# An output of lane X gives way to the closing of a block where fewer than 28 groups of scores are ready

## The chip, the cores and the metric

The kernel runs on one core of a Trainium2 chip. The metric is the device time of one execution in microseconds; the time of a kernel is the median over its runs. The core has five engines that each work through a queue of their own, in the order in which the program was recorded: TensorE (PE, its weight loads PEld), VectorE (DVE), ScalarE (ACT), GpSimd (POOL) and SyncE (SP), which here issues nearly all DMAs.

## What is computed

Four images of 128 channels and 64x64 pixels go through two layers. The first is a convolution block with a selective scan (Mamba), the second attention over the 4096 pixels of an image with 4 heads of 32, and a mixture of 8 experts of which each pixel takes 2:

```python
x = x + _L0_conv_ref(_gn(x), ...)          # norm, 3x3 conv, gelu, scan over 4096 steps, projection
t = _to_tokens(x)
t = t + _L1_attn_ref(_ln_t(t), W_qkv, b_qkv, W_proj, b_proj)
t = t + _L1_ffn_ref(_ln_t(t), router_w, router_b, expert_w, expert_b)
x = _from_tokens(t, x)
```

Attention of one image needs the whole first layer of that image: the scores of a query block against a key block can be made as soon as both blocks have left the scan and were projected. The output of a query block (projection, routing, experts) can be made when all eight key blocks of 512 pixels have been summed.

## The kernel before

An image (a batch b) is cut into 8 blocks of 512 pixels. The instructions of all engines are written down by one Python loop (line 1362), and `queued` (line 389) fixes that order on each engine, so the loop is the schedule. One pass of the loop is a slot. Two slots make a unit: a scan over two of the 16 states of half the channels of a block. A block has 2 x 8 units, so 32 slots; the 32 blocks of the four images fill 1024 slots (`END`). Each block of 32 slots in the loop is called a block of the loop below, with a slot in it from 0 to 31.

Beside the scan, a slot takes three kinds of work:

- One group of scores from the generator `attention` (line 912): two key tiles against 1024 queries of one head. Four matmuls make the scores (`sc`), two exponentials follow (`pT`, in `exponentials`), and in the next slot four matmuls, recorded by the profiler as eight, sum the values (`av`, in `weighted`). There are 1024 groups. `RUNS` fixes their order: pairs of query blocks against ranges of key blocks. A part is one head of such a pair against one or two key blocks, 2 or 4 groups. `ready` (line 908) asks whether the blocks that a part needs have been closed; where they have not, the generator yields nothing and the slot goes without scores. The keys, queries and values of a part are loaded from DRAM, for the next part three groups ahead where it is ready by then.
- Steps of lane Y (up to two per slot): the norm, the convolution and the inputs of the scan of the coming blocks, in a fixed order. At the sixth block of an image the group statistics of the next image come too.
- Steps of lane X (up to two per slot): closings and outputs. A closing (`closed`, line 793) takes the block that the scan has just left through the projections, and stores its keys, queries and values; it is put at the head of the lane as soon as the scan of the block has ended, about slot 2 of the next block of the loop, and takes ten slots. An output (`finished`, line 1032) takes a query block whose sums are complete through projection, routing and the 8 experts, in sixteen slots. Outputs are appended to the lane by `inverted` (line 1012).

Lane X runs one task at a time. `advance` (line 1254) lets an output start only in slots 2 to 17 of a block of the loop:

```python
if (
    tasks[0][0][0] == "out" and slot < END + 4
    and not 2 <= slot % (2 * NST) < NST + 2
):
    return False
```

In slot 2 the scan's last product of the old block has not been handled yet, so an output that waits is taken first, in slots 2 to 17, and the closing of the block follows in slots 17 to 26. Where no output waits, the closing starts in slot 3. After slot 1024 there is no scan; the loop goes on until the remaining scores, closings and outputs are done, with outputs on both lanes. Followed through the counters of the loop, the recorded program has 1194 slots, of which 170 take no scores: slots 0 to 78, 83 to 110, 131 to 142 and 199 to 206 at the start, 383 to 384, 653 to 654 and 911 to 912 where one image's attention gives way to the next, 409 to 412, 469 to 476, and the last 25.

Of the kernel before, what the change touches and what calls it, by code (L numbers as in the profile page):

```python
# [21 lines left out]
NT = BLK // P  # L22
IMG = 64
DI = 64
NST = 16
# [11 lines left out]
def conv_mamba_attn_moe_kernel(ctx: ExitStack, tc: tile.TileContext, t: dict):  # L37
# [374 lines left out]
    def mm(out, lhsT, rhs, start=True, stop=True):  # L412
        tensor.matmul(out, lhsT=lhsT, rhs=rhs, start=start, stop=stop)
# [456 lines left out]


    STEP = 2

    def queries(b, qp, h):

        qs = att.tile([P, 2 * BLK], F32R, name="qs", bufs=2)
        src = kqv[b][1][qp][DH * h : DH * h + DH].rearrange("d a r l -> (d a r) l")
        sync.dma_start(out=qs.bitcast(F32), in_=src)
        return qs

    def keys(b, h, k, u, n):

        ks = att.tile([P, 2 * BLK], F32R, name="ks", bufs=3)
        src = kqv[b][0][k][DH * h : DH * h + DH].rearrange("d a l -> (d a) l")
        src = src[:, u * BLK : (u + n) * BLK]
        sync.dma_start(
            out=ks[:, : n * BLK].bitcast(F32),
            in_=src[:, None, :].to_broadcast([2 * DH, 2, n * BLK]),
        )
        return ks  # L890

    def values(b, h, k, u, n):
        v = att.tile([P, 2, NT, 2 * DH], F32, name="v", bufs=3)
        sync.dma_start(
            out=v[:, :n].rearrange("p i j d -> p i (j d)"),
            in_=kqv[b][2][k][h, u : u + n].rearrange("i p q -> p i q"),
        )
        return v
# [9 lines left out]
    def ready(b, part):  # L908
        last = max(2 * part[0] + 1, 2 * part[2] + part[3] + part[4] - 1)
        return all(("closed", b, i) in done for i in range(last + 1))  # L910

    def attention(b):

        seen, parts = {}, []
        for q, lo, hi in RUNS:
            known = seen.get(q, 0)
            seen[q] = known + hi - lo  # L920
            cuts = [lo, *range(lo + 2 - lo % 2, hi, 2), hi]
            for h in range(NH):
                for k0, k1 in zip(cuts, cuts[1:]):
                    parts.append((
                        q, h, k0 // 2, k0 % 2, k1 - k0, k0 == lo, k1 == hi, known > 0,
                        seen[q] == NB,
                    ))
        assert all(n == NB for n in seen.values())

        def load(part, qs=None):  # L930
            q, h, k, u, n = part[:5]
            if qs is None:
                qs = queries(b, q, h)
            return qs, keys(b, h, k, u, n), values(b, h, k, u, n)

        prev = None
        ahead = None
        for at, part in enumerate(parts):
            q, h, k, _, n, first, last, more, final = part
            if ahead is None:  # L940
                while not ready(b, part):
                    yield None
                ahead = load(part)
                for _ in range(2):
                    yield None
            qs, ks, v = ahead
            ahead = None
            for g in range(0, NT * n, STEP):
                if g == 0 and last:
                    prev = None  # L950
                    if more:
                        prev = att.tile([P, BLK], F32, name="prev", bufs=2)
                        sync.dma_start(out=prev, in_=partial.pop((b, q, h)))
                if g >= NT * n - 3 * STEP and ahead is None and at + 1 < len(parts):
                    nxt = parts[at + 1]
                    if ready(b, nxt):
                        ahead = load(nxt, qs if nxt[:2] == (q, h) and not nxt[5] else None)
                scs = []
                for j in range(g, g + STEP):
                    sc = ps_sc.tile([P, 2, BLK], F32, name="sc")  # L960
                    for u in range(2):
                        mm(
                            sc[:, u, :], ks[:, j * P : (j + 1) * P],
                            qs[:, u * BLK : (u + 1) * BLK],
                        )
                    scs.append((v[:, j // NT, j % NT, :], sc))
                yield (
                    b, q, h, scs, first and g == 0, last and g + STEP == NT * n, prev, final,
                )
# [11 lines left out]
    def weighted(group):  # L981
# [4 lines left out]
        for k, (v, pT) in enumerate(pTs):  # L986
            for u in range(2):
                mm(
                    av[64 * u : 64 * u + 2 * DH, :], v, pT[:, u, :],
                    first and k == 0, last and k == STEP - 1,  # L990
                )
# [262 lines left out]
    def advance(lane, second):  # L1254

        if inside[lane] != second:
            return False
        while True:
            if lane not in running:

                tasks = lanes[lane] if lanes[lane] or slot < END else lanes["X"]
                if tasks and lane == "Y" and tasks[0][0][0] == "closed":
                    return False
                if not tasks or not all(k in done for k in tasks[0][2]):
                    return False

                if (
                    tasks[0][0][0] == "out" and slot < END + 4
                    and not 2 <= slot % (2 * NST) < NST + 2
                ):  # L1270
                    return False
                key, stages, _ = tasks.popleft()
                running[lane] = key, stages(lane) if callable(stages) else stages
            key, stages = running[lane]
            try:
                next(stages)
                inside[lane] = not second
                return True
            except StopIteration:
                assert not second  # L1280
                done.add(key)
                del running[lane]

    def until(key):
        while key not in done:
            flush()
            count = len(done)
            moved = [
                advance(*half) for half in (("X", True), ("Y", False), ("Y", True), ("X", False))
            ]  # L1290
            assert any(moved) or len(done) > count, key
            if ("y0", *blocks[1]) in done:
                next(weights, None)
# [17 lines left out]
    for k in range(-2, len(blocks)):  # L1311
        if 0 <= k:
            b, i = blocks[k]
            Y.append((("in", b, i, 1), inputs(b, i, 1), [("scan", *blocks[k - 1], 1)] if k else []))
        if k + 2 < len(blocks):
            b, i = blocks[k + 2]
            if k + 2 == 0 or i > 0:
                upper(k + 2)
        if 0 <= k + 1 < len(blocks):
            b, i = blocks[k + 1]  # L1320
# [12 lines left out]
    def attention_groups():  # L1333
        for b in range(B):
            yield from attention(b)
        left.clear()
# [6 lines left out]
    h_of, slot = {}, 0  # L1343
# [18 lines left out]
    while (  # L1362
        slot < END or due or closing or summing or waiting or left or later or lanes["X"] or running
    ):
        at, odd = divmod(slot, 2)
# [13 lines left out]
        if summing:  # L1379
            summed_up(*summing)  # L1380
            summing = None
        advance("X", True)
        group = next(groups, None)
        if group:
# [3 lines left out]
        if unit and odd:  # L1388
            hc = read(h, rows.pop((at, 1)))
            late = 2 * (unit[3] == 0)  # L1390
            due.append((slot + 1 + late, unit, 0, hc[:, 0, :], False))
            due.append((slot + 2, unit, 1, hc[:, 1, :], ends(unit)))
        advance("Y", False)
        while closing and closing[0][0] <= slot:
            summing = turned_back(*closing.popleft()[1:])
# [133 lines left out]
```

## Time and profile before

| what | us |
|---|---|
| median of 3 runs | 5179.66 (5176.39 to 5188.5) |
| the profiled execution's own time | 5183.13 |
| its span, first to last instruction | 5180.9 |
| PE busy in the span | 4710.1 |
| DVE busy | 3835.8 |
| ACT busy | 3745.7 |
| POOL busy | 423.1 |

The granted TensorE clock is 0.957 of full speed on average. The span is measured from the first to the last instruction of the profiled execution; the own time of that execution is 2.2 us longer. Nearly all instructions carry line 406, that of the helper which records them, so groups are told apart by their tiles: `sc`, `pT` and `av` are attention, `h` and `hc` the scan, `ps_X` and `ps_Y` the two lanes' PSUM tiles, `xin`, `zs`, `delta`, `du` the inputs. In a line of busy time by windows stand the window, its length, then busy us and instructions of PE, PEld, DVE, ACT and POOL, the granted clock, the DMA share and GB/s. In a line of the timeline stand start, length, the instructions, and in brackets the idle time of the engine before them and what ended it.

### The profile page before, as it was taken

Reading aid. Unit: us, or ns where it says so; the run is one execution under the profiler, and the core shown is the slowest. Engines: PE = TensorE matmul, PEld = TensorE weight load, DVE = VectorE, ACT = ScalarE, POOL = GpSimd, SP = SyncE. Lnnn points to the kernel's source line nnn. Section 1 sums busy time; section 2 is a strip of 40 time slices with the busy share of each in tenths; the row PEclk is TensorE's granted clock in tenths of the full one; section 3 lists DMA queues with packets and bytes.
Section 4 is the critical chain, followed back from the end, with each engine's and each line's share of the span. In section 5 each row is a group of like instructions: output and inputs, shape, how many; then the busy total and the mean of one; then the engine's idle time right before and its main releaser. Section 6 shows DMA issues by size and latency. Waiting matters only on the chain.

```text
span 5180.9 us, 62597 instructions
## 1 busy us (share of the span) xinstructions
PE 4710.1 (91%) x20684; PEld 2321.9 (45%) x20684; DVE 3835.8 (74%) x5780; ACT 3745.7 (72%) x5700; POOL 423.1 (8%) x483
## 2 busy tenths in 40 slices
PE   4567898999999998899999999999999999999997
PEld 2334444444444444444444444444444444443443
DVE  6987767877778887878788887888788877751332
ACT  4556777787787787688888787788777787656543
POOL 1111111100000000101000000000000001000000
PEclk7778999999999999899999999999999999999998
DMA  3556667677666766767766766777766666754542
GB/s 127 183 186 212 205 212 253 233 239 243 229 224 225 239 227 234 242 230 258 252 228 227 238 229 231 258 231 255 265 227 233 221 230 221 262 179 156 184 134 72
DMA packets 451693, 1131.70 MB, mean 218 GB/s; under 512 B 51858, under 2 KB 135331, under 8 KB 451363
## 3 DMA queue, kind: packets, MB, share of 16 engines
q1 hardware_dynamic: 447296, 1125.96, 64.3%
q8 instruction: 166, 2.72, 0.2%
q10 hardware_dynamic: 4066, 1.67, 0.1%
q14 instruction: 165, 1.34, 0.1%
HBM read 967.22 MB, written 143.39 MB: 214 GB/s over the span
## 4 chain that ended last, share of the span: by engine, by line
PE 59%; DVE 19%; ACT 10%; DMA 6%; issue 4%; POOL 2%; SPq 1%; DVEq 0%; ACTq 0%; POOLq 0%
PE av L406 25%; PE sc L406 14%; PE ps_X L406 9%; DVE h L406 6%; PE ps_Y L406 6%; PE y L406 5%; ACT pT L406 3%; ACT L406 2%; DVE hc L406 2%; DMA ks<-kd 2%; ACT xt L406 1%; DVE stX L406 1%; DVE du L406 1%; DMA rows<-bcd 1%; DVE cm L406 1%
## 5 line engine op out<-in xcount | busy, mean ns | idle before, releaser
L406 ACT ACTIVATE pT<-sc 128x1024 f32<-128x1024 f32 x2048 | 1984.3, 1022 | 934.3 <-PE sc L406 932.8
L406 PE MATMUL av<-pT,v 128*64 128x512 f32 x8192 | 2002.8, 610 | 10.8 <-DVE avs L406 10.8
L406 PE MATMUL sc<-qs,ks 128*128 128x512 f32 x4096 | 1302.7, 437 | 75.9 <-ACT pT L406 39.4
L406 DVE TENSOR_TENSOR_SCAN h<-da,state,h 128x1025 f32<-128x1025 f32 x512 | 1204.5, 2353 | 96.6 <-ACT h L406 62.8
L406 PEld LDWEIGHTS sc<-qs,ks 128*128 128x128 f32 x4096 | 703.1, 190 | 812.7 <-ACT pT L406 273.2
L406 PEld LDWEIGHTS av<-pT,v 128*64 128x64 f32 x8192 | 500.4, 137 | 845.7 <-issue 816.7
L406 ACT ACTIVATE da<-delta,amat 128x512 f32<-128x512 f32 x1024 | 742.9, 730 | 1.9
L406 PE MATMUL y<-ident,hc 128*128 128x128 f32 x4096 | 626.2, 284 | 64.6 <-DVE hc L406 64.6
L406 DVE TENSOR_TENSOR hc<-rows,h 128x1024 f32<-128x1024 f32 x512 | 624.6, 1220 | 15.3 <-PE y L406 5.4
L406 DVE TENSOR_TENSOR h<-rows,du 128x1024 f32<-128x1024 f32 x512 | 623.9, 1218 | 13.0 <-DMA rows<-bcd 8.5
L406 PEld LDWEIGHTS y<-ident,hc 128*128 128x128 f32 x4096 | 524.2, 147 | 229.0 <-issue 80.8
L406 ACT ACT_TABLE_LOAD x319 | 409.3, 1283 | 19.5 <-DVE zs L406 14.3
L406 POOL TENSOR_TENSOR rsX<-rsX,mhalf 128x4 f32<-128x4 f32 x92 | 203.7, 2214 | 2504.4 <-DVE rsX L406 2420.4
L406 POOL TENSOR_TENSOR rsY<-rsY,mhalf 128x4 f32<-128x4 f32 x100 | 130.7, 1307 | 2072.5 <-DVE shiftY L406 1561.5
L406 DVE TENSOR_TENSOR avs<-av,prev 128x512 f32<-128x512 f32 x96 | 66.2, 689 | 256.7 <-PE av L406 235.0
L406 PE MATMUL ps_X<-share,w_ew 128*128 128x512 f32 x432 | 213.9, 617 | 9.1 <-DVE share L406 8.8
L406 ACT ACTIVATE xt<-ps_Y,shiftY,rsY 128x128 f32<-128x128 f32 x380 | 143.6, 468 | 81.7 <-POOL shiftY L406 73.8
L406 DVE TENSOR_TENSOR share<-share,xf 128x1024 f32<-128x1024 f32 x128 | 156.0, 1219 | 16.5 <-DMA share<-sharesX 11.7
L406 ACT COPY state<-h 128x2 f32<-128x2 f32 x448 | 88.8, 198 | 92.0 <-DVE h L406 92.0
L406 DVE SCALAR_TENSOR_TENSOR cm<-y,w_fc1w,cm 128x512 f32<-128x512 f32 x195 | 145.1, 744 | 8.0 <-ACT y L406 4.5
L406 PE MATMUL ps_Y<-pairs,inxc 128*128 128x512 f32 x256 | 132.6, 643 | 15.5 <-DMA pairs<-xn 9.9
L406 PEld LDWEIGHTS ps_X<-share,w_ew 128*128 128x128 f32 x432 | 73.2, 189 | 147.0 <-issue 97.1
(248 smaller groups left out, 3437.2 us busy)
## 6 DMA issues: line engine op xcount, KB each, us to landing
rows<-bcd SPq DMA_DIRECT2D x1024, 512.0 KB
ks<-kd SPq DMA_DIRECT2D x192, 512.0 KB
qs<-qd SPq DMA_DIRECT2D x161, 512.0 KB
share<-sharesX SPq DMA_DIRECT2D x108, 512.0 KB
v<-vd SPq DMA_DIRECT2D x192, 256.0 KB
ks<-kd SPq DMA_DIRECT2D x128, 256.0 KB
avd<-avs SPq DMA_DIRECT2D x96, 256.0 KB
prev<-avd SPq DMA_DIRECT2D x96, 256.0 KB
```

The costliest lines, as they stand in the source:

```text
L406: return lambda *args, **kw: queued(op(*args, **kw))
```

## The change

An output may now start in slots 2 to 17 only if `stocked(28)` holds as well. `stocked` walks the parts of the attention from the one that is being recorded (`position`) and counts the groups of those that are ready, 2 or 4 a part. It returns true when 28 are reached or the image's parts end, and false when it meets a part that is not ready. It also returns true where attention has not begun and at the first part of an image that waits for its first blocks. Where it is false, the output waits at the head of lane X; when the scan ends, the closing is put ahead of it.

```diff
     STEP = 2
+    LEAD = NST + 12
...
+    position = [None]
+
+    def stocked(wanted):
+
+        if position[0] is None:
+            return True
+        b, parts, at = position[0]
+        if at == 0 and not ready(b, parts[0]):
+            return True
+        for part in parts[at:]:
+            if not ready(b, part):
+                return False
+            wanted -= NT * part[4] // STEP
+            if wanted <= 0:
+                return True
+        return True
...
         for at, part in enumerate(parts):
             q, h, k, _, n, first, last, more, final = part
+            position[0] = b, parts, at
...
                     tasks[0][0][0] == "out" and slot < END + 4
-                    and not 2 <= slot % (2 * NST) < NST + 2
+                    and not (2 <= slot % (2 * NST) < NST + 2 and stocked(LEAD))
                 ):
                     return False
```

## The prediction

> **What bounds the kernel now.** I read the page first, for the engines' shares and the slices of the span.
>
> ```profile
> span 5180.9 us, 62597 instructions
> PE 4710.1 (91%) x20684; PEld 2321.9 (45%) x20684; DVE 3835.8 (74%) x5780; ACT 3745.7 (72%) x5700; POOL 423.1 (8%) x483
> PE   4567898999999998899999999999999999999997
> PEclk7778999999999999899999999999999999999998
> ```
>
> The matmul engine is busy in nine tenths of nearly every slice after the first five. VectorE and ScalarE stand at 74% and 72%, so in the middle of the span it is TensorE's own queue that sets the pace; its idle time is what a reordering can win or lose. The dip in the sixteenth and seventeenth slice (1943 to 2202 us), where the clock falls too, is the first place to look.
>
> Next I followed the slot counter through the recorded program (it holds no time) and set each group of scores beside its exponentials in the trace, so that a slot has a start in us. The scores pause, apart from the start (slots 0 to 142, 199 to 206) and the batch changes (383 to 384, 653 to 654, 911 to 912), in two runs: slots 409 to 412 and 469 to 476, twelve slots in all. The loop has 1024 slots with a scan; the scores that are left over run after it, in slots 1024 to 1168. So I asked for busy time by windows: two stretches of that tail in which nothing but scores runs, then pairs of stretches with the same work, with a pause and without one.
>
> ```profile
> 4693.00:4765.00 72.00, 72.00 (x290) 27.78 (x288) 3.46 (x5) 46.68 (x49) 0.00 (x0) 1.00 0.42 141
> 5027.60:5075.50 47.90, 47.90 (x194) 18.52 (x192) 0.00 (x0) 31.61 (x34) 0.00 (x0) 1.00 0.26 83
> ```
>
> Columns: window, its length, busy us of PE, PEld, DVE, ACT, POOL, the granted clock, DMA share, GB/s. TensorE is never idle here. The first window is 24 groups, the second 16: 72.0 / 24 = 3.00 and 47.9 / 16 = 2.99 us a group. That is what a slot at the end costs.
>
> ```profile
> 1769.40:1796.80 27.40, 17.84 (x73) 8.89 (x70) 18.24 (x18) 18.31 (x29) 0.00 (x0) 0.86 0.88 278
> 1911.60:1939.50 27.90, 26.66 (x113) 12.50 (x110) 18.68 (x19) 25.23 (x36) 0.00 (x0) 1.00 0.84 274
> 2044.70:2095.70 51.00, 30.80 (x120) 16.89 (x119) 44.56 (x71) 23.21 (x41) 6.60 (x4) 0.71 0.79 262
> 3205.20:3260.60 55.40, 48.14 (x208) 23.63 (x207) 43.20 (x69) 37.65 (x57) 5.66 (x4) 0.94 0.85 307
> ```
>
> The first two are slots 23 to 28 of blocks 12 and 13 (a block being 32 slots), with the same closing and the same inputs beside them; only the first has the four-slot pause. It is 0.5 us shorter, though PE has 8.8 us less to do in it. The other two are slots 19 to 28 of blocks 14 and 22, both with a closing, inputs and the next batch's group statistics: eight empty slots save 4.4 us. The pauses hardly shorten the main loop, and each empty slot comes back later at 3 us. What sits in the first pause:
>
> ```profile
> 1785.51 1.04 PE L406 MATMUL y<-ident,hc 128*128 128x128 f32 x8
> 1793.21 1.11 PE L406 MATMUL y<-ident,hc 128*128 128x128 f32 x4 [6.67 <-DVE hc L406]
> 1795.59 1.62 PE L406 MATMUL sc<-qs,ks 128*128 128x512 f32 x3 [1.26 <-DMA ks<-kd]
> ```
>
> TensorE stands for 6.7 us, then for another 1.3 us until keys land that could only be asked for once the closing had stored them.
>
> **What the Trainium skill says.** Perfetto Trace Analysis, section Identifying the Most-Contended Engine, warns that matmul busy share is no measure of peak; I therefore use idle time before PE, not its 91%. TensorE: Matmul & The Clock Gate, section Part 1 (the HAM clock gate), puts the clock at half after an idle window of some 3.4 us and says full clock returns with sustained work; the windows agree, 0.86 and 0.71 in the pauses against 1.00 and 0.94 without. Its section Architectural detail calls VectorE and ScalarE strict first-in-first-out queues, so a product of an output that waits for its transfer holds the scan behind it; the trace of before has DVE idle 60.7 us before aT, in 20 of 32 cases. ScalarE: Activation LUTs, section What ACT_TABLE_LOAD costs, prices a table load at about 1283 ns; the page has the same mean for 319, and the two recorded programs hold the same number, so I give it no weight.
>
> **The change part by part.** (1) Nothing is added or removed: counted by operation and tiles, both recorded programs hold the same instructions on all five engines. The same slot count on the changed program gives 1182 slots for 1194. The pauses at 409 to 412 and 469 to 476 are gone; those at the start and at the batch changes stay (two slots each, now at 641 and 899). So 133 groups are left for the tail in place of 145.
>
> (2) Tail: 12 slots x 2.993 us = -35.9. They come out of the stretch between the last closing and the first outputs of the last batch (slots 1051 to 1089 before, 1052 to 1077 after), which is pure scores, so nothing else hides there. The last attention groups and the last two outputs keep their distance to the end. Slots 1026 to 1051 are rearranged (the closing now ahead of one output), at 111.83 us PE busy of 113.1: same work, 0 +- 2.
>
> (3) The 12 pauses filled: +0.5 us and, just after, +0.7 (three slots of block 12 take 19.86 us for 20.56 elsewhere, while TensorE catches up) = +1.2; block 14 by its pair with block 22, +4.4 and +0.5 after it (88.85 against 89.39 for the next 20 slots) = +4.9. Sum +6.1. The bounds are 0 and +12: 12 x 3.0 = 36 us of PE work minus the idle time it falls into.
>
> (4) Moved: eight closings of the main loop (batch 1: blocks 3, 4, 5, 7; batch 2: 3, 5, 7; batch 3: 5; recorded in blocks 12, 13, 14, 16, 20, 22, 24 and 30 of the loop) start at slot 3 of that block for slot 17, and the output beside each at slot 12 for slot 2. A closing runs over ten slots and issues one load and seven stores of 2.5 MB together; an output runs over sixteen and issues three loads of 256 KB, four shares of 512 KB, and two stores. All of them now stand between other rows and keys in SP's queue. There is no block with that order in the trace, but its halves are there:
>
> ```profile
> 2402.20:2451.20 49.00, 46.32 (x216) 23.16 (x215) 38.41 (x67) 39.56 (x63) 7.62 (x8) 1.00 0.64 213
> 1813.30:1859.20 45.90, 43.93 (x209) 22.39 (x208) 35.16 (x67) 39.48 (x61) 3.45 (x7) 1.00 0.58 197
> 1888.00:1936.20 48.20, 46.79 (x218) 23.27 (x217) 37.33 (x64) 43.39 (x67) 6.53 (x6) 1.00 0.72 244
> 1308.70:1358.00 49.30, 46.48 (x216) 23.27 (x215) 40.12 (x72) 41.89 (x64) 3.84 (x4) 1.00 0.70 235
> ```
>
> Slots 2 to 11 with a closing (block 17) leave TensorE idle 49.00 - 46.32 = 2.7 us, with an output (block 13) 2.0. Slots 18 to 27 with an output (block 9) leave 2.8, with a closing (block 13) 1.4. Together +0.7 and +1.4 = +2.1 a block. Of block 9's 2.8, 1.4 us comes from inputs (inv) still landing right after they were made, which an output held back for ten slots does not meet; without it +0.7. I take the middle, +1.4, for eight blocks: +11.2. Bounds: -4 (the idle time before the routing chain is covered by other work) and +26 (3.3 a block, all of block 9's). Blocks 14 and 22, with group statistics, have no pair; they get the same figure.
>
> Sum: -35.9 + 6.1 + 11.2 = -18.6. On this execution's span: 5180.9 - 18.6 = 5162.3. Its own time is 5183.13, 2.2 above its span and 3.5 above the median of the runs, so the median goes from 5179.66 to about 5161. I say 5160.
>
> **The rivals.** Two per mille, about 10.4 us, is what a measurement of this kernel can tell from no change.
>
> A, the forecast: pauses filled at little cost, the moved blocks give back a third. 5160, own range 5150 to 5169.
>
> B, the moved order is free: closings beside the first half of a block find as much room as beside the second. For it: TensorE is idle only 3.4 us in a plain block, and the total work is the same. Then -35.9 + 6.1 = -29.8, with up to -40 if the filling is free too: 5140 to 5150, say 5148.
>
> C, nothing to see: the freed 30 us go to new waits. Attention is 4, then 12 groups further on in all later blocks, so its key loads, its partial sums (prev) and its batch changes meet other transfers. In before such meetings cost 1.2 to 3 us each plus half clock for 3 to 10 us (the clock falls about twenty times after 1200 us). Ten more would do it. Against it: as many can go as come. 5170 to 5190, say 5178.
>
> D, slower: the transfer pile-up. In a moved block the closing's 2.5 MB of stores leave in slots 8 to 13, and the output's three loads (aT, inv, acc) queue behind them in slot 12 with only three slots, about 13 us, until VectorE takes them in order, the scan behind it. In block 9 inv took 12.0 us, and DVE stood 4.1 us. If each moved block loses over 3.7 us, the gain is gone; over 5.0 it is a loss that can be told. At 6 us: 8 x 6 - 29.8 = +18, 5198. Against it: the DMA share in a moved block is what it was, near 0.7.
>
> That the change doesn't do what it says: the slot count shows that it does.
>
> **How the numbers follow.** A 0.50, B 0.30, C 0.14, D 0.06. Faster: A and B, 0.80; within 0.2%: C, 0.14; slower: D, 0.06. The range, 5140 to 5178, takes in B whole, A, and the better half of C; it leaves out D and the rest of C.
>
> **What would show it.** The tail after the last scan shorter by 12 groups of 2.99 us, with windows of pure scores unchanged at 2.99. No half-clock stretch in blocks 12 and 14, whose slots 19 to 28 should take 55 us for 51. TensorE idle in a moved block about 4.8 us for 3.4; if it is 3.4, B holds, if over 7, D. DVE's idle time before aT should stay near 61 us; well above 100 speaks for D. I am wrong if the tail keeps its length, or if blocks whose order did not change get slower.

## The result: 5161.6 us for 5179.7

The changed kernel takes 5161.63 us (median of 9 runs, 5157.54 to 5169.97) against 5179.66 us (9 runs): a ratio of 0.9966, interval 0.9958 to 0.9975, so 13 to 22 us faster. The forecast was 5160. The profiled execution has a span of 5158.6 us, 22.3 us under that of the kernel before. First the page of the changed kernel: shares, and the slices of busy TensorE and of its clock.

```profile
span 5158.6 us, 62573 instructions
...
PE 4703.0 (91%) x20684; PEld 2317.3 (45%) x20684; DVE 3835.7 (74%) x5780; ACT 3743.0 (73%) x5700; POOL 433.5 (8%) x483
...
PE   4567898999999999999999999999999999999997
...
PEclk7778999999999999999999999999999999999997
```

The counts of matmuls, VectorE and ScalarE instructions are those of before (the 24 instructions fewer are semaphore instructions), and the dip in the sixteenth and seventeenth slice is gone, in the clock too. Then busy time by windows: the pure scores of the tail after the last closing, slots 23 to 28 of block 12, slots 19 to 28 of block 14.

```profile
4699.90:4771.80 71.90, 71.90 (x290) 27.78 (x288) 4.21 (x8) 46.53 (x49) 0.00 (x0) 1.00 0.47 156
1765.50:1797.30 31.80, 31.80 (x123) 14.71 (x122) 21.06 (x20) 25.55 (x36) 0.00 (x0) 1.00 0.68 210
2047.50:2101.10 53.60, 49.95 (x201) 23.15 (x200) 46.77 (x65) 35.85 (x53) 1.48 (x1) 0.97 0.80 269
```

The same stretch of the tail before is slots 1052 to 1087:

```profile
4693.00:4800.70 107.70, 107.70 (x434) 41.67 (x432) 6.24 (x10) 69.74 (x72) 0.00 (x0) 1.00 0.46 156
```

107.7 - 71.9 = 35.8 us: twelve groups of 2.99, as the forecast had it. The two pauses are full: block 12's stretch is 4.4 us longer and TensorE is never idle in it, block 14's 2.6 longer. The rest of the difference between two single executions holds scatter: up to the start of block 12 the two programs are the same, and the changed kernel's execution is already 3.8 us ahead there; after the last group of scores it takes 5.6 us longer.

### The profile page after: what moved, and what is told of

It reads as the page before. It is cut to its first block, busy times and chain, and to the rows that moved or that the text cites. A ratio compares the mean times of both kernels' runs of the same rounds, so it can differ in the third digit from the quotient of the medians.

```text
span 5158.6 us, 62573 instructions
## 1 busy us (share of the span) xinstructions
PE 4703.0 (91%) x20684; PEld 2317.3 (45%) x20684; DVE 3835.7 (74%) x5780; ACT 3743.0 (73%) x5700; POOL 433.5 (8%) x483
## 4 chain that ended last, share of the span: by engine, by line
PE 58%; DVE 17%; ACT 11%; DMA 7%; issue 4%; POOL 2%; SPq 1%; DVEq 0%; ACTq 0%; POOLq 0%
PE av L406 25%; PE sc L406 14%; PE ps_X L406 9%; PE ps_Y L406 6%; PE y L406 6%; DVE h L406 6%; ACT pT L406 4%; ACT L406 3%; DMA ks<-kd 2%; DVE hc L406 2%; DMA rows<-bcd 1%; ACT xt L406 1%; POOL rsX L406 1%; DMA inv<-inverse 1%; DVE stX L406 1%
## 5 line engine op out<-in xcount | busy, mean ns | idle before, releaser
L406 DVE TENSOR_TENSOR hc<-rows,h 128x1024 f32<-128x1024 f32 x512 | 624.4, 1220 | 15.7 <-PE y L406 5.4
L406 DVE TENSOR_TENSOR share<-share,xf 128x1024 f32<-128x1024 f32 x128 | 155.9, 1218 | 23.5 <-DMA share<-sharesX 13.9
L406 DVE TENSOR_TENSOR res<-res,ps_X 128x512 f32<-128x512 f32 x108 | 73.7, 683 | 99.9 <-PE ps_X L406 99.7
L406 PE MATMUL ps_Y<-pairs,inxc 128*128 128x512 f32 x256 | 131.2, 638 | 15.8 <-DMA pairs<-xn 10.2
```

Of the source, the lines that this page charges most:

```text
L406: return lambda *args, **kw: queued(op(*args, **kw))
```

## The experiments

Times are medians; each ratio is to the kernel before on the same chip. In the tables of windows below a block runs from its slot 1 to slot 1 of the next, so that its lane tasks fall into it whole.

**The move alone.** Lanes as in the changed kernel, scores as in the kernel before. This separates the order of closing and output from the filled pauses and from attention's new place.

```diff
+    MOVED = (12, 13, 14, 16, 20, 22, 24, 30, 32)
...
-                    and not (2 <= slot % (2 * NST) < NST + 2 and stocked(LEAD))
+                    and not (
+                        2 <= slot % (2 * NST) < NST + 2
+                        and not (slot // (2 * NST) in MOVED and slot % (2 * NST) == 2)
+                    )
...
-        group = next(groups, None)
+        held_back = 409 <= slot <= 412 or 469 <= slot <= 476
+        group = None if held_back else next(groups, None)
```

> Closings and outputs stand as in the changed kernel, slot for slot, but the scores are held back in slots 409 to 412 and 469 to 476, so that every group of scores stands in its slot of before. This is the move alone, without the filled pauses and without the shift of attention. Theory T (a moved block costs 4 to 8 us because the output's loads queue behind the closing's stores; the blocks that were not moved got faster only because attention was shifted): slower than before by 18 to 28 us, 5198 to 5208, and the unmoved blocks take as long as before. The forecast's figure of 1.4 us a block: 5191. Rival R (the moved lanes themselves made the neighbouring blocks faster): within 5 us of before.

5192.81 for 5184.69, ratio 1.0016 (1.0010 to 1.0023): 8 us slower, 5 to 12. That is near the forecast's figure (11), not theory T's 18 to 28, and just outside the 5 of rival R. The blocks tell more. The kernel before in blocks 13, 16, 24 and 30:

```profile
1809.80:1953.30 143.50, 140.10 (x642) 69.51 (x642) 115.96 (x175) 117.77 (x183) 11.67 (x15) 1.00 0.70 235
2254.70:2398.80 144.10, 140.47 (x642) 69.42 (x641) 118.69 (x180) 116.78 (x181) 12.20 (x14) 1.00 0.72 243
3419.60:3563.20 143.60, 140.26 (x641) 69.37 (x640) 116.78 (x178) 116.83 (x181) 11.60 (x14) 1.00 0.73 243
4295.50:4450.70 155.20, 143.84 (x633) 69.76 (x633) 119.10 (x171) 114.59 (x174) 15.73 (x9) 0.97 0.71 244
```

And with the eight closings moved:

```profile
1817.40:1964.50 147.10, 140.92 (x642) 69.18 (x641) 117.45 (x176) 117.24 (x183) 15.82 (x15) 1.00 0.68 229
2259.60:2407.60 148.00, 141.80 (x641) 69.89 (x640) 119.22 (x180) 116.45 (x180) 14.38 (x14) 0.99 0.73 237
3430.90:3578.80 147.90, 140.84 (x641) 69.12 (x640) 117.03 (x178) 116.39 (x180) 15.14 (x14) 1.00 0.70 236
4309.50:4459.20 149.70, 140.41 (x633) 68.58 (x632) 118.83 (x171) 114.21 (x175) 14.88 (x9) 1.00 0.76 255
```

Length minus PE busy is TensorE's idle time. In blocks 13, 16 and 24 it goes from 3.4 to 6.2, from 3.6 to 6.2 and from 3.3 to 7.1, and the block takes 3.6 to 4.3 us longer; block 20 does the same (5.6 us). In block 30 it falls from 11.4 to 9.3, the clock comes back to 1.00, and the block is 5.5 us shorter; blocks 14 and 22, read the same way, are 5.9 and 4.3 shorter. Most blocks that were not moved agree to 0.4 us, so a single block can be compared, though some near the pauses and batch changes scatter by 1 to 2 us, and block 14 by more: with the order of before it takes 157.3 us here, but 153.8 to 154.0 in the traces of three of the runs below, so some 3.4 of its 5.9 us are chance.

Of the five plain blocks only 20 and 24 have TensorE waiting over 0.5 us for the output's first product (`aT`), 3.0 and 1.7 us. In 12, 13 and 24 it waits 1.6 us for VectorE's `cm` at about slot 16, and in 16 and 20 2.4 and 2.7 us for keys.

**Nine plain blocks moved.** To make the cost large, from the kernel before, with `MOVED = (18, 19, 20, 21, 23, 26, 27, 28, 29)` and nothing held back.

> The kernel before, with nine other closings put ahead of their output, all in plain blocks of the loop: 18, 19, 20, 21, 23, 26, 27, 28 and 29. No pause is filled and every group of scores stands in its slot of before. Theory T: 4 to 6 us a block, 36 to 54 in all, so 5215 to 5234. The forecast's figure of 1.4 a block: 5192. If the move is free: 5180.

5227.89, ratio 1.0084 (1.0072 to 1.0096): 43.5 us, 4.8 a block. In a plain block the move costs three times what the forecast took. The profiled execution was 9.6 us under the median; in it the nine blocks are 31.5 us longer, 3.5 each. Where in a block the loss lies shows in slots 12 to 17 of block 27, before and moved:

```profile
3911.40:3940.20 28.80, 28.78 (x123) 13.93 (x122) 28.45 (x37) 18.15 (x31) 1.69 (x2) 1.00 0.77 259
```
```profile
3936.50:3967.60 31.10, 26.93 (x128) 14.99 (x127) 25.80 (x44) 18.62 (x33) 3.96 (x3) 0.89 0.70 231
```

Before, TensorE and VectorE are both busy throughout. Moved, TensorE stands for 4.2 us and then works at a lower clock. Over the nine blocks its idle time goes from 21 to 23 us in slots 2 to 11, from 11 to 34 in slots 12 to 17, and from 14 to 6 in slots 18 to 27; with the same work it is also busy 13.5 us longer. The queue of SP in block 27 (start, length, DMA), without the lines before and between:

```profile
3932.40 0.54 SPq L406 DMA_DIRECT2D qd<-hi  x1
3933.19 0.53 SPq L406 DMA_DIRECT2D qd<-lo  x1
...
3937.79 0.53 SPq L406 DMA_DIRECT2D aT<-total  x1
3938.36 0.69 SPq L406 DMA_DIRECT2D inv<-inverse  x1
3939.10 0.97 SPq L406 DMA_DIRECT2D acc<-td  x1
3940.18 0.52 SPq L406 DMA_DIRECT2D vd<-vst  x1
```

and the chain of waits of the same stretch (start, length, what):

```profile
3937.79 7.87 DMA aT<-total
3945.66 3.74 issue
3949.39 0.70 DVE aT L406
3950.10 0.04 issue
3950.14 2.07 PE ps_X L406 x8
```

The output's loads are issued 4.6 us after the closing's queries, among stores; aT lands 7.9 us later, the chain loses 3.7 us more to something that it doesn't name, and only then VectorE makes the product for which TensorE stands. The timeline gives that matmul an idle time of 4.15 us, released by aT. VectorE too does nothing for 4.7 us before that product. This is the wait that rival D named, and 4.8 us a block is near the 5 at which it would have been a loss that can be told. In the whole trace TensorE waits 22.1 us for this product in lane X's outputs, against 2.5 before. That the stores in front delay the loads is argued from the order in the queue; the next runs test it.

**The output later.** If the stores in front of the loads are the whole cause, four slots between them should help.

```diff
-                    and not (2 <= slot % (2 * NST) < NST + 2 and stocked(LEAD))
+                    and not (
+                        2 <= slot % (2 * NST) < NST + 2 and stocked(LEAD)
+                        and not 4 <= slot % (2 * NST) < NST
+                    )
```

> The changed kernel, but an output that gave way starts at slot 16 of its block for slot 12, four slots after the closing's last store. Theory T (its loads come late behind the stores, VectorE waits for them and TensorE behind it in slots 14 to 18): the 3 to 4 us of idle TensorE in slots 12 to 17 of the eight moved blocks go, 12 to 25 us in all, 5137 to 5150. Rival R (the loss lies in the closing's place beside the inputs of the scan, in slots 3 to 12): no change, 5158 to 5166. If the output then collides with the inputs in slots 24 to 27 and stays beyond them: slower than the changed kernel.

5169.33 for 5184.69, ratio 0.9968 (0.9957 to 0.9980), no different from the changed kernel's 0.9966. By blocks it is not nothing: 16, 20 and 24 gain 3.3, 4.0 and 2.4 us on the changed kernel, but block 22 loses 7.8. The same start on the nine plain blocks:

```diff
-                        and not (slot // (2 * NST) in MOVED and slot % (2 * NST) == 2)
+                        and not (slot // (2 * NST) in MOVED and slot % (2 * NST) < NST)
```

> The nine moved closings in plain blocks again, but each output that gave way starts at slot 16 of its block for slot 12. If the loss of 43 us comes from the output's loads queueing behind the closing's stores: 10 to 20 us above before. If it comes from the closing's place in slots 3 to 12, or the output just collides elsewhere: 35 to 45 above before, as with the start at 12.

5211.84 for 5180.30, ratio 1.0064 (1.0050 to 1.0078): 33 us for 43. The intervals touch, and 33 is nearer to the 35 to 45 of the rival than to the 10 to 20 of the theory. So at most a part of the cost is the meeting of stores and loads. In the traces the wait for the aT product falls from 22.1 to 4.6 us, yet the nine blocks together are no shorter (1334.7 us for 1336.0) and TensorE's idle time in them is 65 us for 64, and 46 before: waits of some 1.3 us for other tiles, at about slots 17 and 26 of most of these blocks, come in its place. The 2.1 us for which TensorE waits for lane Y's norm in slot 8 of eight of the blocks are there in both; before, it waits 1.8 us for the output's routing a little later in six of the nine. The lengths hardly differ, but in each of the two runs the clock falls to half for 3.4 us after five of the eight longer waits, and before after none of these six.

**The output waits longer for its loads.** Two more slots between the loads and the product of aT, in outputs that gave way.

```diff
         yield
         yield
         yield
+        if slot < END and slot % (2 * NST) > 8:
+            for _ in range(4):
+                yield
         vector.tensor_mul(aT, aT, inv)
```

> The changed kernel, but an output that gave way waits two slots more between its three loads and the product of aT. Theory T in its narrow form (VectorE, in order, is held by the late inv): the waits of 1 to 2 us before the first product go, and the waits for keys stay: 4 to 10 us less, 5152 to 5158. If the whole loss hangs on that product: 5140 to 5150. Rival R: no change, 5158 to 5166.

5168.96 for 5184.69, ratio 0.9972 (0.9962 to 0.9981): as the changed kernel. Again some blocks win (12 and 13: 2.3 and 3.2 us) and others lose (22: 4.2, 24: 2.2).

The traces tell blocks apart. In 12 and 13 of the changed kernel TensorE waits for the aT product (1.1 and 1.5 us), and the longer wait takes that away. In 16, 20, 22 and 24 it waits 1.8 to 3.7 us for keys of the next scores, which are asked for after the closing's stores and the output's loads; with the longer wait these become 4.7 to 6.0. The scores of slot 15 of block 24, in the changed kernel, with the output at slot 16, and with the longer wait:

```profile
3499.27 1.36 PE L406 MATMUL sc<-qs,ks 128*128 128x512 f32 x4 [3.64 <-DMA ks<-kd]
```
```profile
3506.09 1.16 PE L406 MATMUL sc<-qs,ks 128*128 128x512 f32 x4 [0.96 <-DMA ks<-kd]
```
```profile
3510.16 1.62 PE L406 MATMUL sc<-qs,ks 128*128 128x512 f32 x3 [5.99 <-DMA ks<-kd]
```

With the output's loads out of the way the wait shrinks to a quarter. So of the plain blocks the later start helps those in which keys are due there most, and the longer wait those in which none are; block 22, with group statistics, loses by both.

**Three blocks moved.** `MOVED = (14, 22, 30)`, and only slots 469 to 476 held back.

> The kernel before with three closings put ahead of their output, those of blocks 14, 22 and 30 of the loop, in which lane Y comes to the inputs of the scan five slots earlier (slots 19 to 21). Scores are held back in slots 469 to 476, so every group stands in its slot of before. Theory P (a moved closing costs some 4 us in a plain block and saves some 5 us in these three, read from the run with all eight moved): 15 us faster than before on the same chip, give or take 6. Rival (the gain in these blocks was chance, moves cost about 1 us everywhere): 0 to 5 us slower.

5171.98 for 5180.30, ratio 0.9984 (0.9976 to 0.9992): 8 us faster, 4 to 12, less than the 15 expected and clear of the rival. The trace puts most of it into one block: block 30 takes 149.4 us for 155.2 (154.4 and 155.9 in the two runs with nine moved), block 22 157.3 for 159.2, and block 14 153.8, no less than it takes unmoved in other traces. In these blocks a closing in slots 17 to 26 meets a lane Y that comes to the inputs in slots 19 to 21; moved, the output runs beside it. Which of the waits there is decisive wasn't tried.

**Empty slots in a plain block.** What a slot without scores is worth where TensorE is the bound. From the kernel before:

```diff
-        group = next(groups, None)
+        group = None if 868 <= slot <= 883 else next(groups, None)
```

> The kernel before with scores held back in sixteen slots, 868 to 883, of a plain block in which an output and part of a closing run beside the scan; the sixteen groups come at the end. At the end they cost 16 x 2.99 = 47.9 us. If an empty slot saves what it saved in the two pauses that the change fills (6 us over 12 slots): 40 us slower. If it saves the whole of its TensorE work because TensorE is the bound: no change. VectorE's 118 us of a block's 143 leave room for at most 0.8 us a slot: 35 us slower, which is what I expect.

5225.81 for 5180.30, ratio 1.0082 (1.0068 to 1.0096): 42 us slower, 35 to 50, which doesn't tell the 35 that I expected from 40. (From here on attention stands 16 slots later, which moves other blocks too.) Block 27 before and in this kernel, each followed by its slots 6 to 19:

```profile
3861.90:4005.40 143.50, 140.05 (x642) 69.49 (x641) 117.76 (x177) 116.86 (x180) 11.60 (x14) 1.00 0.67 223
3888.70:3949.20 60.50, 58.66 (x267) 29.00 (x267) 57.73 (x96) 43.70 (x72) 3.15 (x7) 1.00 0.66 217
```
```profile
3865.50:4006.80 141.30, 106.05 (x449) 55.62 (x448) 117.69 (x177) 87.47 (x148) 11.60 (x14) 0.86 0.57 198
3891.30:3951.50 60.20, 33.29 (x114) 19.47 (x115) 57.77 (x96) 21.49 (x46) 3.16 (x7) 0.68 0.46 165
```

Sixteen groups fewer, and the block is 2.2 us shorter. Over the block VectorE is busy 118 of 141 us, which looks like room; but in slots 6 to 19 it is busy 57.7 of 60.5 us before and 57.8 of 60.2 without scores. Both engines are full there, so taking work from TensorE alone saves next to nothing. And of the 47.9 us of scores that left, TensorE's busy time fell by only 34.0: with the gaps the mean clock of these slots went down to 0.68, and the matmuls that stayed took longer.

**One pause filled.** All eight closings moved, only slots 409 to 412 held back.

> All eight closings moved, but scores held back in slots 409 to 412, so only the pause of eight slots is filled. Theory: the eight slots give 8 x 2.99 = 23.9 us at the end and cost 5 to 6 us where they are filled, so 18 us under the run with all eight moved and none filled (0.16% above before): a ratio of 0.9981. The four other slots then bring the rest, 8 us. Rival (a fill costs as much as it gives, and the changed kernel's gain comes from attention's other phase): 1.0016 as with none filled.

5176.67 for 5181.52, ratio 0.9988 (0.9981 to 0.9994): by the two ratios about 14.5 us under the run with none filled, for 18 expected, and nowhere near the rival. In the trace block 14 takes 5.5 us longer than with its pause, which is the forecast's 4.9.

**Starts chosen by block.** The gains of single blocks put together: start at slot 16 in blocks 16, 20 and 24, the longer wait in 12 and 13, the rest as in the changed kernel.

```diff
-                    and not (2 <= slot % (2 * NST) < NST + 2 and stocked(LEAD))
+                    and not (
+                        2 <= slot % (2 * NST) < NST + 2 and stocked(LEAD)
+                        and not (
+                            slot // (2 * NST) in (16, 20, 24)
+                            and 4 <= slot % (2 * NST) < NST
+                        )
+                    )
...
+        if slot // (2 * NST) in (12, 13):
+            for _ in range(4):
+                yield
         vector.tensor_mul(aT, aT, inv)
```

> The changed kernel with a start of the moved outputs chosen by block from the traces of the last runs: at slot 16 in blocks 16, 20 and 24, two more slots of waiting before the aT product in blocks 12 and 13, as in the changed kernel in 14, 22 and 30. If the gains of single blocks add up (2.4 to 4.0 us in each of five blocks): 15 us below the changed kernel, a ratio to before of 0.9937. If they are scatter of single executions: 0.9966 as the changed kernel.

5144.90 for 5180.30, ratio 0.9933 (0.9919 to 0.9946). It was repeated beside the changed kernel in another set of runs:

> The kernel with the output's start chosen by block, on another chip: if its 17 us below the changed kernel are no accident of one chip, a ratio of 0.992 to 0.9945, clear of the changed kernel's; if they are, 0.9966.

> The changed kernel once more, beside the two that follow, so that all three stand on one chip: a ratio to before of 0.9958 to 0.9975, as before.

5147.69 against 5159.55 for the changed kernel and 5181.52 for the kernel before: ratios 0.9931 (0.9918 to 0.9945) and 0.9954 (0.9940 to 0.9967). (The changed kernel itself came out a little better than the 0.9958 to 0.9975 expected.) The kernel with chosen starts is faster than both, by 12 to 17 us than the changed kernel, though in the second set the two intervals just touch. Blocks 13, 16 and 24 in the changed kernel, and here:

```profile
1811.00:1958.80 147.80, 140.63 (x641) 69.26 (x641) 116.61 (x176) 117.32 (x182) 13.78 (x15) 1.00 0.68 228
2259.10:2411.60 152.50, 144.32 (x641) 71.06 (x640) 120.44 (x182) 115.98 (x180) 13.64 (x14) 0.97 0.69 238
3431.40:3582.80 151.40, 142.75 (x641) 70.01 (x640) 118.34 (x180) 116.11 (x180) 16.25 (x14) 0.99 0.71 240
```
```profile
1815.60:1961.10 145.50, 140.50 (x641) 69.41 (x641) 117.11 (x176) 117.04 (x182) 13.10 (x15) 1.00 0.70 232
2260.10:2409.50 149.40, 143.20 (x641) 70.19 (x640) 120.31 (x182) 115.95 (x179) 14.79 (x14) 0.98 0.73 243
3427.40:3576.40 149.00, 140.59 (x641) 69.67 (x640) 118.31 (x180) 116.02 (x180) 14.64 (x14) 1.00 0.73 242
```

Each is 2.3 to 3.1 us shorter, much as it was where only its start or only its wait was altered.

## Why the prediction was right, step by step

(1) and (2), nothing but places change, and twelve slots of pure scores leave the tail: 35.8 us measured for 35.9. The windows of pure scores stayed at 2.99 us a group.

(3), the filled pauses: +6.1 was too little. From the run with all eight moved and none filled to the changed kernel, block 12 grows by 4.2 and block 14 by 5.8 us, 10.0 together and inside the bound of 12. The term for block 14 held (4.9, and 5.5 with that pause alone filled): the pair was well chosen, and its lines show why so little is saved, VectorE being busy 44.6 of 51.0 us in the pause. The term for block 12 did not: its pair, block 13, had a closing in slots 23 to 28, while in the changed kernel the output's expert products stand there. The stretch with TensorE busy throughout is 31.8 us, not 27.9. (A slip that changes no sum: the 19.86 and 20.56 us are those of six slots, 29 to 34, not of three.)

(4), the move: +11.2 for eight blocks, 8 measured. The sum held and its parts did not. Five plain blocks cost 18.3 us together in the trace with the eight moved (0.8, 3.6, 4.0, 5.6 and 4.3 in 12, 13, 16, 20 and 24), against 7.0 at 1.4 each; the three others gave back 15.7, some 3.4 of it the chance in block 14, where I had put the same cost for want of a pair. Runs with one kind alone have the same signs: +4.8 and -2.8 us a block. In the plain blocks the step that failed was to compare slots 2 to 11 and 18 to 27 and to put the six slots between at nothing, without a reason. The halves were read well: in the four plain blocks with full scores (13, 16, 20 and 24) a closing in slots 2 to 11 leaves TensorE idle 2.3 to 2.7 us, for the 2.7 read from block 17, and an output in slots 18 to 27 leaves 0.6 to 1.3, less even than the discounted 1.4. But in slots 12 to 17, where closing and output meet, idle time goes from 5 to 16 us over the five blocks, and in block 20 the clock is at half for 10 us after them. What TensorE waits for there differs: the aT product, keys, or `cm`.

Sum with measured terms: -35.8 + 10.0 + 8 = -17.8, and the medians differ by -18.0. That it met the forecast's -18.6 is partly luck: the filling was 4 us dearer, the move 3 us cheaper.

What the forecast named as marks: no half clock at full pauses, shown (0.97 in block 14 for 0.71, 1.00 in block 12 for 0.86). Slots 19 to 28 of block 14 at 55 us: 53.6. TensorE idle in a moved plain block at 4.8, and over 7 for D: 7.2 in block 13, 8.2 in 16, 8.7 in 24. So the size that D feared was real in the plain blocks, at its break-even of 3.7 us or above (18.3 us over five, 43.5 over nine); its mechanism is only a part of it, since the wait for aT went with the later start and the loss largely stayed. It failed as a forecast because three of the eight blocks are not of that kind. DVE's idle time before aT, which I had named as its mark, was 51.5 us for 60.7: the wrong place to look, for outputs that were not moved wait there too; TensorE's weight loads behind aT waited 15.8 us for 4.2. Rival C, new waits from attention's other place: between the run with eight moved and none filled and the changed kernel, blocks 18, 25 and 26 are 4.7, 4.4 and 3.6 us shorter, 16, 24 and 30 are 4.5, 3.4 and 3.9 longer. It moves single blocks as far as feared (most of block 30's gain is lost again), and the sum from block 13 on, without 14, is about -1 us.

## What to carry to other kernels

A slot that a planned loop leaves empty in its middle is paid for at its end at the full rate of whatever runs there, and saves almost nothing where it stands if another engine is full there as well: 12 slots gave 36 us and cost 10. Shares of the whole span hide this; VectorE is busy 74% of it, but 95% of slots 6 to 19, most of those that were emptied. Price such a move by a stretch with the same work beside it, not only the same tasks in the block, and leave no stretch out: the six slots between the two that the forecast compared cost most. A later start removed the wait that was seen and brought others, so count what a fix saves in the whole block. A rule for all blocks averages winners and losers: chosen by block, the same moves were worth another 12 to 17 us.

## What was not expected of the hardware

Some blocks whose order was left alone repeat to 0.1 us in separate executions (block 27: 143.50 and 143.50), while stretches with waits on transfers scatter by several (block 14: 157.3 and 153.8). The clock adds to each such wait: the same 633 recorded matmuls of block 30 kept TensorE busy 143.84 us at a mean clock of 0.97 and 140.41 at 1.00, so 3.4 of the 5.5 us that the move gained there are the clock's. The forecast took an idle window of some 3.4 us for the fall of the clock; in the trace of before single waits of 1.86, 2.02 and 2.81 us (they end at 2474.5, 1420.4 and 4403.6 us) are each followed by 3.4 us at a clock of 0.50, while one of 1.82 us (3901.9) is not.
